# Attention steps taken as output, values, scores instead of scores, values, output

## The chip, the cores and the metric

The kernel runs on one core of a Trainium2 chip. The metric is device time in microseconds of one execution. Before the change it is 1657.19 us, the median of 10 runs from 1653.45 to 1661.23.

## The reference

A batch of 16 sequences, each of 128 tokens of width 256, goes through four layers. Each layer adds a gated cross attention over a context of the same shape and then a gated feed-forward part, all in float32:

```python
x = x + tanh(g_xattn[0]) * L0_xattn(ctx, layernorm(x), ctx)      # 16 heads of 16
x = x + tanh(g_ffn[0])   * L0_ffn(layernorm(x))                  # 8 experts, top 2, gelu
x = x + tanh(g_xattn[1]) * L1_xattn(layernorm(x), ctx, ctx)      # 16 heads of 16, biases
x = x + tanh(g_ffn[1])   * L1_ffn(layernorm(x))                  # dense plus 8 LoRA experts
x = x + tanh(g_xattn[2]) * L2_xattn(ctx, ctx, layernorm(x), mask)  # 16 heads of 16, key mask
x = x + tanh(g_ffn[2])   * L2_ffn(layernorm(x))                  # 8 experts, top 2, swiglu, and a shared one
x = x + tanh(g_xattn[3]) * L3_xattn(ctx, layernorm(x))           # 8 heads of 64, keys of both
x = x + tanh(g_ffn[3])   * L3_ffn(layernorm(x))                  # 8 experts, top 2, silu
```

An attention is the projection of queries, keys and values, scores, a softmax over the keys (in layer 1 over the other axis of the scores), the product with the values, and an output projection. Only the order in which the sequences of an attention pass through these parts is changed.

## The kernel before

**Stages.** The residual x lies in the core's memory as 16 tiles of 128 x 256, one per sequence (b). Four sequences make a block (blk), and layer norm, the query and key projections and the routers work on blocks, with 512 tokens at once. The program runs: attention of layer 0 with part of its experts' slots, the rest of these slots, attention of layers 1 and 2 in one loop (the feed-forward part of layer 1 goes along with it), the shared expert and the slots of layer 2, attention of layer 3, and its slots. A slot is 128 tokens that go to one expert.

**The attention loop.** `attend` (from L1303) walks over steps, one per sequence, in three parts. `scores` (L1184 for layers 0 to 2, L1970 for layer 3) projects the values of sequence b (`ps_v`, L942 or L948), copies them out on VectorE, multiplies keys and queries on TensorE into four PSUM banks (`ps_s`, L1212), and takes exp of the four banks on ScalarE into four tiles `e` (L1222, L1227); in layer 1 VectorE also sums e (L1236), inverts the sums and scales the values. `values` (L1255, L1995) multiplies e with the values and, in layers 0, 2 and 3, with ones for the sums (`ps_o`, L1267, in layer 3 `ps_sum` too, L2002); then VectorE takes a reciprocal (L1278, L2011) and a product (L1280, L2021) into `oT`. In layer 1 ScalarE only copies (L1275). GpSimd adds the reciprocals to a running sum (L1081), with which the program later checks that none was out of range. `output` (L1284, L2027) projects oT (`ps_y`, L1288, L2031), adds it to x on VectorE (L366) and starts the statistics of x there (L245, L246).

At iteration n the loop calls scores of step n, values of step n-1, and output of step n-2, in this order. On TensorE, ScalarE and VectorE the program's order is the order of execution (`IN_ORDER`, L1299): an instruction that waits holds up all behind it on its engine.

**Jobs between the parts.** Each part calls `tick` at certain points: scores three times (after the values' copy, halfway through the scores' matmuls, after exp), values twice (before and after the end of its vector work), output once at its end. A tick lets every running job (a Python generator) go on to its next yield, after as many ticks as it asked for. Jobs are the preparation of the next block (`ahead`, at every fourth n: layer norm, transposes, queries, keys), and what follows a finished block (`behind`, after the output of its fourth sequence: the router of a mixture layer, or layer 1's whole feed-forward part). With n equal to the number of steps, `late` is set and a filler starts, a longer job of expert matmuls (slots of layer 0, the shared expert of layer 2, slots of layer 3), which runs on behind the attention. At a block's begin, the loop runs ticks until the block's preparation is done.

**Buffers.** Four PSUM banks (pool `ps_mm`, L100) hold the scores; four more (pool `ps_x`, L101) go in turn to everything else: values projection, values, output, transposes, query and key projections. A new user waits until the user four allocations before is done with its bank. There are nine tiles `e`, three tiles for the values of a sequence, and two of `oT`.

## Time and profile before

| what | us |
|---|---|
| median of 10 runs | 1657.19 |
| the profiled execution | 1657.35 |
| its span, first to last instruction | 1655.5 |
| TensorE busy | 1538.0 (93%) |
| VectorE busy | 876.2 (53%) |
| ScalarE busy | 636.9 (38%) |
| GpSimd busy | 327.1 (20%) |

In this profile PE is TensorE, PEld its loading of weights, DVE VectorE, ACT ScalarE, POOL GpSimd and SP the queue that issues most DMAs. L with a number is a line of the kernel. "ps_y L1288 <- DVE oT" says that the instruction of line 1288 that writes ps_y waited for VectorE's writing of oT. The attention steps of layer 0 lie between 21 and 161 us of the span, those of layers 1 and 2 between 447 and 730, and those of layer 3 between 1248 and 1495. [...]

### The profile page before, as it was taken

How to read it: one execution, taken by the hardware profiler on the slowest of the kernel's cores; microseconds unless marked ns; L12 is line 12 of the kernel's file. 1: busy time of each engine (PE TensorE's matmuls, PEld its weight loads, DVE VectorE, ACT ScalarE, POOL GpSimd, SP SyncE). 2: the span in 40 equal slices, each digit the busy share in tenths (PEclk: the TensorE clock that was granted, in tenths of full speed). 3: DMA queues.
4: the chain of work that ended last, by engine and by line, in shares of the span. 5: the costliest groups of instructions: out<-in, count | busy, mean ns of one | idle time of the engine just before them, and what ended most of it. 6: DMA issues, size and time to landing. Idle time of an engine off the chain costs nothing.

```text
span 1655.5 us, 34913 instructions
## 1 busy us (share of the span) xinstructions
PE 1538.0 (93%) x12803; PEld 1195.9 (72%) x12803; DVE 876.2 (53%) x2850; ACT 636.9 (38%) x1517; POOL 327.1 (20%) x412
## 2 busy tenths in 40 slices
PE   6998999999988999999999999999989999998891
PEld 4677889999455666655559999999846665677791
DVE  3676322422367756764445555556724535557664
ACT  4455423345355555553225333334543323222110
POOL 4123411111600000221100111011150002023433
PEclk8998999999999999999999999999989999999996
DMA  9606575342600000110064414310360000034855
GB/s 337 232 28 217 187 255 171 127 145 89 118 2 1 1 15 14 40 40 26 26 219 151 152 42 139 118 33 28 100 118 1 14 1 27 1 115 133 279 171 185
DMA packets 111273, 169.68 MB, mean 102 GB/s; under 512 B 17130, under 2 KB 84527, under 8 KB 111089
## 3 DMA queue, kind: packets, MB, share of 16 engines
q1 hardware_dynamic: 86224, 112.38, 21.6%
q0 software_dynamic: 20304, 49.66, 9.5%
q10 hardware_dynamic: 4560, 5.25, 1.0%
q8 instruction: 108, 1.77, 0.5%
q14 instruction: 77, 0.62, 0.1%
HBM read 268.81 MB, written 48.18 MB: 191 GB/s over the span
## 4 chain that ended last, share of the span: by engine, by line
PE 58%; DVE 8%; ACT 4%; DMA 3%; issue 1%; POOL 0%; SPq 0%; DVEq 0%; POOLq 0%; ACTq 0%
PE ps_w L1598 16%; PE ps_w L1533 6%; PE ps_qk L1855 5%; PE ps_e L823 5%; PE ps_v L1964 3%; PE ps_g L1646 2%; PE ps_u L1646 2%; PE ps_s L1985 2%; PE ps_o L1267 2%; PE ps_y L2031 2%; PE ps_s L1555 2%; PE ps_o L2002 1%; DVE sums L1236 1%; PE ps_router L413 1%; PE ps_q L933 1%
## 5 line engine op out<-in xcount | busy, mean ns | idle before, releaser
L1598 PEld LDWEIGHTS ps_w<-xT,w 128*128 128x128 f32 x2304 | 264.0, 192 | 2.5
L1598 PE MATMUL ps_w<-xT,w 128*128 128x128 f32 x2304 | 264.9, 275 | 0.0
L835 POOL DMA_INDIRECT yd<-y,to x117 | 119.2, 1019 | 560.0 <-DVE c L798 306.9
L823 PE MATMUL ps_e<-w,hT 128*128 128x256 f32 x848 | 197.6, 380 | 2.2 <-DVE hT L1503 1.3
L823 PEld LDWEIGHTS ps_e<-w,hT 128*128 128x128 f32 x848 | 154.5, 190 | 21.4 <-DVE hT L1503 2.3
L1606 ACT ACTIVATE u<-ps_w,b 128x128 f32<-128x128 f32 x312 | 89.5, 368 | 172.5 <-PE ps_w L1598 165.3
L1609 DVE SCALAR_TENSOR_TENSOR m<-ps_w,b,u 128x128 f32<-128x128 f32 x312 | 87.8, 345 | 110.9 <-PE ps_w L1598 93.9
L1421 PE MATMUL ps_h<-xT,w 128*128 128x128 f32 x1120 | 134.9, 280 | 6.3 <-DMA w<-in_l_w_dram 4.1
L1421 PEld LDWEIGHTS ps_h<-xT,w 128*128 128x128 f32 x1120 | 132.9, 196 | 9.4 <-issue 3.8
L1426 ACT ACTIVATE hT<-ps_h,b 128x128 f32<-128x128 f32 x312 | 89.3, 373 | 117.1 <-issue 83.4
L524 POOL DMA_INDIRECT xg<-xn,xi x96 | 94.1, 980 | 153.6 <-ACT u L1539 55.0
L1533 PE MATMUL ps_w<-xnT,sw 128*128 128x512 f32 x256 | 111.8, 593 | 0.0
L831 DVE SCALAR_TENSOR_TENSOR y<-ps_e,c,bias 128x256 f32<-128x256 f32 x78 | 37.7, 483 | 125.5 <-PE ps_e L823 124.3
L1081 POOL TENSOR_TENSOR sum_range<-sum_range,rs 128x256 f32<-128x256 f32 x48 | 35.2, 733 | 343.9 <-DVE rs L1278 157.5
L1533 PEld LDWEIGHTS ps_w<-xnT,sw 128*128 128x128 f32 x256 | 47.9, 190 | 57.3 <-issue 50.9
L1278 DVE RECIPROCAL rs<-ps_o 128x256 f32<-128x256 f32 x32 | 56.2, 1756 | 45.5 <-PE ps_o L1267 43.6
L306 ACT ACTIVATE xn<-x,nmr,rstd 128x256 f32<-128x256 f32 x128 | 67.8, 598 | 31.1 <-DVE nmr L302 30.3
L788 DVE COPY xT<-ps_xr 128x256 f32<-128x256 f32 x117 | 48.6, 418 | 57.4 <-PE ps_xr L786 57.3
L1212 PE MATMUL ps_s<-qM,kT 32*128 32x256 f32 x768 | 68.9, 421 | 5.6 <-ACT e L1227 5.6
L1227 ACT ACTIVATE e<-ps_s 128x512 f32<-128x512 f32 x128 | 65.8, 602 | 11.4 <-PE ps_s L1212 11.4
L815 ACT ACTIVATE bias<-b,c 128x256 f32<-128x256 f32 x78 | 40.4, 518 | 67.0 <-DVE c L801 26.6
L1855 PE MATMUL ps_qk<-kvx,w_att 128*128 128x512 f32 x128 | 62.9, 625 | 0.6 <-DVE kvx L1842 0.6
(276 smaller groups left out, 2559.5 us busy)
## 6 DMA issues: line engine op xcount, KB each, us to landing
w<-in_l_w_dram SPq DMA_DIRECT2D x156, 1024.0 KB
w<-in_l_w_dram SPq DMA_DIRECT2D x39, 512.0 KB
kT<-in_l_wgu_dram SPq DMA_DIRECT2D x39, 512.0 KB
xg<-zeros POOLq DMA_DIRECT2D x15, 1170.0 KB, 25.6
xr<-xg SPq DMA_DIRECT2D x78, 130.0 KB
b<-in_l_b_dram SPq DMA_DIRECT2D x78, 128.0 KB
kT<-in_l_w_dram SPq DMA_DIRECT2D x39, 256.0 KB
x<-yd POOLq DMA_DIRECT2D x48, 128.0 KB, 4.8
```

The lines of the kernel that those rows point to most:

```text
L306: nc.scalar.activation(xns[:, i, 0:D], src, AF.Identity, bias=nmr[:, i:i + 1], scale=rstd[:, i:i + 1])
L524: self.unordered(nc.gpsimd.indirect_dma_start(out=xg[:, :], in_=xns[:, i, :], in_offset=None, out_offset=bass.IndirectOffsetOnAxis(ap=xi[: ...
L823: nc.tensor.matmul(po, lhsT=hT[:, f, :], rhs=lane(s)["w2"][:, f, :], start=(f == 0), stop=(f == nf - 1),)
L835: self.unordered(nc.gpsimd.indirect_dma_start(out=yd[:, :], in_=y, in_offset=None, out_offset=bass.IndirectOffsetOnAxis(ap=to[:, 0:1], axi ...
L1212: nc.tensor.matmul(pss[j][:, 2 * c:2 * c + 2, :], lhsT=self.kT[blk][part, c, tok], rhs=self.qM[blk][part, c, :, tok], start=True, stop=True,)
L1421: nc.tensor.matmul(ps[:, i, :], lhsT=w["w1"][:, k, f * P:(f + 1) * P], rhs=xT[:, k, :], start=(k == 0), stop=(k == KC - 1),)
L1426: nc.scalar.activation(hT[:, f, :], ps[:, i, :], AF.Gelu, bias=w["b1"][:, f:f + 1])
L1533: nc.tensor.matmul(ps, lhsT=wt[:, k, f * P:(f + 1) * P], rhs=xnT[:, k, :], start=(k == 0), stop=(k == KC - 1),)
L1598: nc.tensor.matmul(ps[:, f, :], lhsT=wt[:, k, s, f * P:(f + 1) * P], rhs=xT[:, k, :], start=(k == 0), stop=(k == KC - 1),)
L1606: nc.scalar.activation(u[:, f, :], pair[0][:, f, :], AF.Identity, bias=w["b1"][:, i:i + 1])
L1609: nc.vector.scalar_tensor_tensor(m1[:, f, :], pair[1][:, f, :], w["b3"][:, i:i + 1], u[:, f, :], ALU.add, ALU.mult,)
L1855: nc.tensor.matmul(ps, lhsT=w[:, k, c * P:(c + 1) * P], rhs=src[:, k, :], start=(k == 0), stop=(k == KC - 1),)
```

## The change

The three parts of an iteration come in the opposite order, and with one more step between them: output of step n-3, values of step n-2, scores of step n. The loop runs one iteration longer, and the point from which the filler runs moves by one iteration. A block's preparation still starts, and is still waited for, at the head of the iteration, which is now ahead of output and values instead of directly ahead of scores; what follows a finished block now starts between output and values.

```diff
-            for n in range(len(steps) + 2):
+            for n in range(len(steps) + 3):
                 if n == len(steps) - 1 and open_end:
                     next(filler)
-                if n == len(steps):
+                if n == len(steps) + 1:
                     late = True
...
+                if n >= 3:
+                    att, b = steps[n - 3]
+                    att.output(b, tick)
+                    if b % BPB == BPB - 1:
+                        _, _, behind, blk = blocks[(n - 3) // BPB]
+                        jobs.append([behind(blk), 0])
+                if 2 <= n < len(steps) + 2:
+                    att, b = steps[n - 2]
+                    att.values(b, tick)
+                if n < len(steps):
                     att, b = steps[n]
                     att.scores(b, tick)
-                if 1 <= n <= len(steps):
-                    att, b = steps[n - 1]
-                    att.values(b, tick)
-                if n >= 2:
-                    att, b = steps[n - 2]
-                    att.output(b, tick)
-                    if b % BPB == BPB - 1:
-                        _, _, behind, blk = blocks[(n - 2) // BPB]
-                        jobs.append([behind(blk), 0])
```

## The prediction

> **What bounds the kernel now.** I read the busy time by stretch first, for the four attention stages, since the change touches nothing else. The columns are the stretch, its length, and busy microseconds with instruction counts for TensorE, its weight load, VectorE, ScalarE and GpSimd; then granted clock, DMA share and GB/s.

> ```profile
> 21.00:161.00 140.00, 126.44 (x1634) 95.56 (x1634) 94.18 (x296) 72.55 (x152) 32.42 (x39) 0.91 0.52 192
> 434.00:584.00 150.00, 133.44 (x1118) 83.40 (x1122) 101.40 (x274) 77.11 (x164) 18.29 (x30) 0.95 0.10 15
> 584.00:730.00 146.00, 140.77 (x1707) 96.65 (x1704) 94.06 (x265) 79.37 (x140) 27.34 (x32) 1.00 0.10 31
> 1248.00:1498.00 250.00, 242.31 (x2603) 161.21 (x2602) 130.15 (x363) 75.19 (x153) 27.79 (x35) 0.99 0.10 30
> ```

> These are layers 0, 1, 2 and 3. TensorE is idle for 13.6, 16.6, 5.2 and 7.7 us of them: 43 us is all that a reordering could win, and layers 2 and 3 have almost nothing to give. So I next read what ends TensorE's waits (total, times, longest).

> ```profile
> PE ps_ln L329 <- ACT xn L306: 13.9, 8, 4.3
> ...
> PE ps_s L1212 <- ACT e L1227: 5.6, 4, 2.6
> ...
> PE ps_o L1267 <- DVE oT L1280: 3.3, 4, 1.8
> ...
> PE ps_y L1288 <- ACT oT L1275: 1.7, 2, 0.9
> ```

> The first is layer norm of the next block (part of it at 434, before the attention steps); the second, scores waiting for banks that exp still reads. The last two are not data waits: values and output wait for one of the four general PSUM banks, which an earlier values result occupies until oT is written. Adding the smaller rows of that kind (ps_l 1.4, ps_q 1.0 and 0.6 behind VectorE's oT; ps_ln 1.9, ps_zT 0.8 behind ScalarE's) gives 10.7 us. No row has output waiting for its own oT. The timeline of one step of layer 2 tells why (start, length, engine, line, operation):

> ```profile
> 619.65 1.15 PE L1212 MATMUL ps_s<-qM,kT 32*128 32x256 f32 x16
> ...
> 620.73 1.08 PE L1267 MATMUL ps_o<-e,v 128*32 128x128 f32 x32
> ...
> 621.62 1.06 PE L1267 MATMUL ps_o<-e,ones 128*32 128x128 f32 x32
> 622.61 1.13 PE L1288 MATMUL ps_y<-w_att,oT 128*128 128x256 f32 x4
> 622.82 1.76 DVE L1278 RECIPROCAL rs<-ps_o 128x256 f32<-128x256 f32 x1 [1.50 <-PE ps_o L1267]
> ...
> 623.69 1.03 PE L948 MATMUL ps_v<-w_att,ctxT 128*128 128x256 f32 x4
> 624.61 0.42 DVE L1280 TENSOR_TENSOR oT<-ps_o,rs 128x256 f32<-128x256 f32 x1
> 624.65 1.15 PE L1212 MATMUL ps_s<-qM,kT 32*128 32x256 f32 x16
> ```

> Scores, values, output follow each other. From the last values matmul (622.68) to oT written (625.03) is 2.35 us, and that oT is used only after another output, scores and values: at 628.92.

> **The change, part by part.** Nothing is added or removed but an iteration; the numbers of instructions stay. Written out, the old order is S(n) V(n-1) O(n-2) S(n+1) V(n) O(n-1), the new one S(n) O(n-2) V(n-1) S(n+1) O(n-1) V(n). So despite "two" and "three steps ago", what happens is that O and V change places. From exp to values the way grows by one output; from values to output it shrinks from O+S+V to S alone. The steps themselves issue no DMA. POOL's addition of the range watch (0.73 us, one a step) moves with values, and no engine waits for it. The queues of SP and POOL are touched otherwise only through jobs (loads, scatters) that start up to three ticks earlier relative to S, which I cost at nothing: the DMA share is 0.52 in layer 0 and 0.10 after it, and POOL is busy under a quarter of the time; without that cover it would be the 0.52 us that a late row cost at 142.32.

> (a) *Output waits for its own oT.* 2.35 us of VectorE against the scores step in between: in layer 2 from 623.69 to 625.80, 2.11 us, so 0.24 us of wait; in layer 0 the values projection is shorter (121.14 to 122.83, 1.69 us), so 0.66. That holds where no job's matmuls stand between V and O. In the new TensorE order that is 6 steps of layer 0 and 5 of layer 2: 6 x 0.66 + 5 x 0.24 = 5.2 us. Queued behind the waiting output is V(n-1), all of whose inputs are there. Bounds: 2.6 (half covered by other late work) to 11 (each wait 1 us, as output's VectorE tail, 0.48 + 0.43 + 0.18, now stands ahead of the reciprocal).

> (b) *Vector work of the router ahead of the reciprocal.* At 118 to 123 the ranks' nine small operations (about 0.19 each, 1.7 us) delayed it. In the new order such a group falls into the middle of values, where the second half (1.0 us) covers part: 0.8 us in two steps without matmul filler, 1.6. Bounds 0 and 5.0 (twice the 2.52 us from 120.24 to 122.76).

> (c) *The ends of layers 0, 2 and 3.* After the last scores the order is O(13) V(14) O(14) V(15) O(15): O(14) stands directly behind V(14), with no S between, and waits the whole 2.35 us in layers 0 and 2; in layer 3 it is about 0.8, since the reciprocal there runs under values (1264.81 to 1265.58 for the multiply). For layer 0 I take half: the expert work that follows waited there anyway (0.52 us at 142.32 for its rows). 1.2 + 2.35 + 0.8 = 4.3, bounds 0.8 and 5.5. O(15) is covered by a slice of filler (eight passes over the shared expert's weights took 3.54 us at 714.78).

> (d) *Layer norm against exp.* Jobs advance by ticks, so their place among the steps moves: the four normalizations (0.52 each, 2.08) now come ahead of a step's four exps, not behind, and exp frees the score banks later. Walking one block of layer 0 with these durations I get waits of 1.0 (next block's queries) and 0.9 (the job behind), for scores and transposes, and of 0.6 together in layer 2, where a step is longer; for three blocks that is 5.7 and 1.8 us. Against that, the present waits at these places go: 0.85, 0.66, 0.99, 1.73 and 0.88 in layer 0 (5.1) and 0.72 in layer 2. Net +1.7, bounds -5.8 and +8.

> (e) *Layer 1.* Its stalls come from a chain through both other engines: the sums of exp (2.46 us on VectorE), the statistics behind them, then ScalarE, whose oT copy stands in line behind the logarithm that waits for these. Per block before: 0.87 + 0.36 + 1.87 = 3.1 us (485 to 491). In the new order the same chain costs output and transposes some 0.9 + 0.8 to 2.4. For four blocks I take -3, bounds -8 and +6.

> (f) *Layer 3.* 242.31 of 250 us busy, oT 2 us ahead of the scores' end: 0, bounds -2 and +3.

> Where (a) and (d) fall into one step, exp catches up during output's wait: -2. The sum is 5.2 + 1.6 + 4.3 + 1.7 - 3 - 2 = +7.8 us. The profiled execution took 1657.35 (span 1655.5 and 1.85 around it), 0.16 from the median of 1657.19, so the sum gives 1665.

> **Clock.** The values step at 105.69 took 3.25 us to 108.94, the one at 113.23 only 1.96; before the slow one stands a wait of 1.73. A half-speed stretch thus cost 1.3 us, with waits of under 2 us around. Three such stretches more or fewer make 4 us either way: I put that into the range, not the sum. [...]

> **Rivals.** *Faster, 22%:* the change frees banks. Output's bank is emptied before the reciprocal occupies VectorE, so fewer of the four are held. If all 10.7 us of bank waits behind oT go and new waits stay at (a), 5.2, the time is 1651.9. For: these waits exist, above all in layer 1. Against: layer 2, with the same order, has under 3 us of them. It decides once new waits total under 7.4. *Nothing measurable, 15%:* one wait takes another's place, TensorE's idle time stays near 43 us: 1657. "About 0.2%, 3.3 us" is what a measurement of this kernel can tell. *VectorE becomes the bound, 12%:* where its queue is full (the reciprocal started 2.5, 3.1, 5.97 us late in steps of layer 0, and in seven steps of layers 0 to 2 oT was written 1.8 to 2.8 us after the scores behind which output now stands), output waits about 3 us each time: 7 x 3 = 21 us, 1678. Against: in such stretches the rest of TensorE's queue waited too.

> **How the numbers follow.** The forecast, slower by 3.3 to 16, has 51%. Slower is 51 + 12 = 63%, the same 15%, faster 22%. The range 1652 to 1678 leaves out about one in ten on each side: below, the faster rival with more than its price; above, the VectorE rival beyond its price. The likeliest case alone covers 1660.5 to 1674.

> **What would show it.** TensorE waits named output behind oT, VectorE's in layers 0 and 2, several of 0.2 to 0.7 and two of about 2.3 at the ends; the waits behind oT at other matmuls fewer; layer 2's idle time above 8 us; layer 3's the same. I would be wrong if jobs' matmuls fill the gap between V and O more often than I count, or if layer 1's chain shortens by more than a few microseconds.

## The result

The changed kernel takes **1671.03 us** (median of 9 runs, 1668.64 to 1674.48); the kernel before, beside it, 1656.27 (median of 31, 1652.69 to 1663.71). The ratio is **1.0093, 95% interval 1.0080 to 1.0106**: slower by 14.8 us. The forecast was 1665, with 63% on slower; time and sign held. The sum behind it did not hold in its parts, as the experiments show.

**Profile after.** The span is 1667.9 us, 12.4 longer than before. The busy time by stretch, over the same four windows and with the same columns as shown of before:

```profile
21.00:161.00 140.00, 119.70 (x1589) 87.58 (x1588) 94.19 (x285) 65.94 (x138) 32.43 (x39) 0.91 0.52 192
434.00:584.00 150.00, 130.53 (x1030) 78.82 (x1030) 93.16 (x252) 76.90 (x161) 23.27 (x35) 0.93 0.15 22
584.00:730.00 146.00, 141.14 (x1670) 97.89 (x1670) 96.09 (x274) 78.17 (x140) 23.58 (x29) 0.99 0.08 25
1248.00:1498.00 250.00, 244.63 (x2468) 154.77 (x2468) 122.82 (x325) 75.74 (x157) 29.17 (x37) 0.99 0.10 26
```

The windows stand still while the work moves later, so fewer instructions fall into them. Layer 0 shows the change without that: TensorE is busy 119.7 of 140 us, where it was 126.4, and gets 1589 matmuls done instead of 1634. The waits of TensorE say why (total, times, longest):

```profile
PE ps_y L1288 <- DVE oT L1280: 13.9, 14, 3.0
...
PE ps_ln L329 <- ACT xn L306: 8.0, 4, 2.7
PE ps_y L1288 <- DVE sm_m L380: 5.8, 3, 2.5
...
PE ps_y L1288 <- ACT oT L1275: 4.4, 3, 2.8
...
PE ps_s L1212 <- ACT e L1227: 2.4, 2, 2.0
PE ps_y L2033 <- DVE oT L2023: 2.2, 1, 2.2
...
PE ps_y L1288 <- DVE fm_m L398: 1.5, 1, 1.5
...
PE ps_ln L329 <- ACT oT L1275: 1.1, 1, 1.1
```

Five of these rows are output (`ps_y`), 27.8 us together; before, the rows of output came to 2.7 us (2.1 in layers 0 to 2, 0.6 in layer 3), and none was for its own oT. Where the row names `sm_m` or `fm_m`, a small router operation that stands just behind oT on VectorE, it is the same wait: in the timeline below, of layer 2, output starts at 734.11, 0.14 after oT ends at 733.97.

```profile
731.75 1.76 DVE L1278 RECIPROCAL rs<-ps_o 128x256 f32<-128x256 f32 x1 [0.92 <-PE ps_o L1267]
733.54 0.43 DVE L1280 TENSOR_TENSOR oT<-ps_o,rs 128x256 f32<-128x256 f32 x1
733.88 0.18 DVE L380 TENSOR_REDUCE sm_m<-logits 128x4 f32<-128x32 f32 x1
```

```profile
730.53 1.08 PE L1267 MATMUL ps_o<-e,ones 128*32 128x128 f32 x32
734.11 2.04 PE L1288 MATMUL ps_y<-w_att,oT 128*128 128x256 f32 x4 [2.50 <-DVE sm_m L380]
```

Three things went the other way. Of the 10.7 us of waits for a PSUM bank behind an older oT only the 1.1 of the last row above are left (9.6 gone; against that, other matmuls now wait 4.9 us in four rows behind output's addition to x, `DVE x L366`, before 0.4 in one); layer norm's 13.9 became 8.0, and scores behind exp 5.6 became 2.4. So in these rows 27.8 came and 18.7 went, +9.1. TensorE's idle time from the first scores of layer 0 to the last gating matmul of layer 3 says the same: 71.7 us before, 80.6 after (+8.9). The rest of the 12.4 is longer busy time. In sum the clock has no part in it: the time at half clock in that stretch is 68.3 us in both profiles.

For the experiments I use the length of stages, each taken between named instructions, so that it does not depend on where the work lies: layer 0 from its first scores matmul to its last output matmul; layers 1 and 2 with the shared expert from the first scores to the last `ps_w` of the shared expert; layer 3 from the first scores to the last `ps_g` of its slots. Where layers 1 and 2 are named apart, the cut is the end of layer 1's last output matmul. In brackets is the time in which TensorE runs nothing, where it is used. All are of one profiled execution each.

| kernel | layer 0 | layers 1 and 2, shared | layer 3 and its slots |
|---|---|---|---|
| before | 130.0 (12.6) | 411.5 (23.3) | 371.3 |
| after | 135.3 (19.6) | 426.3 (28.1) | 363.4 |

### The profile page after: what moved, and what is told of

Same layout as the page of the kernel before. It is cut to its first block, busy times and chain, and to the rows that moved or that the text cites. A ratio compares the mean times of both kernels' runs of the same rounds, so it can differ in the third digit from the quotient of the medians.

```text
span 1667.9 us, 34882 instructions
## 1 busy us (share of the span) xinstructions
PE 1542.6 (92%) x12803; PEld 1194.9 (72%) x12803; DVE 880.4 (53%) x2850; ACT 633.9 (38%) x1513; POOL 327.1 (20%) x412
## 3 DMA queue, kind: packets, MB, share of 16 engines
q1 hardware_dynamic: 86224, 112.38, 21.3%
## 4 chain that ended last, share of the span: by engine, by line
PE 80%; DVE 11%; DMA 3%; ACT 3%; issue 2%; SPq 1%; POOL 0%; DVEq 0%; ACTq 0%; POOLq 0%
PE ps_w L1600 15%; PE ps_e L823 12%; PE ps_h L1423 7%; PE ps_w L1535 6%; PE ps_qk L1857 5%; PE ps_o L1267 4%; PE ps_v L1966 3%; PE ps_y L1288 2%; PE ps_s L1212 2%; PE ps_s L1987 2%; DVE rs L1278 2%; PE ps_g L1648 2%; PE ps_k L933 2%; PE ps_y L2033 2%; PE ps_router L413 2%
## 5 line engine op out<-in xcount | busy, mean ns | idle before, releaser
L823 PEld LDWEIGHTS ps_e<-w,hT 128*128 128x128 f32 x848 | 154.5, 190 | 22.2 <-DVE hT L1505 2.3
L306 ACT ACTIVATE xn<-x,nmr,rstd 128x256 f32<-128x256 f32 x128 | 68.4, 595 | 45.0 <-DVE nmr L302 45.0
L1288 PE MATMUL ps_y<-w_att,oT 128*128 128x256 f32 x192 | 59.3, 435 | 25.6 <-DVE oT L1280 13.9
L1278 DVE RECIPROCAL rs<-ps_o 128x256 f32<-128x256 f32 x32 | 56.1, 1752 | 30.2 <-PE ps_o L1267 30.1
L1212 PE MATMUL ps_s<-qM,kT 32*128 32x256 f32 x768 | 69.5, 418 | 2.4 <-ACT e L1227 2.4
L1227 ACT ACTIVATE e<-ps_s 128x512 f32<-128x512 f32 x128 | 65.7, 599 | 10.7 <-PE ps_s L1212 10.5
L1288 PEld LDWEIGHTS ps_y<-w_att,oT 128*128 128x128 f32 x192 | 35.6, 205 | 46.5 <-issue 19.7
```

Source lines behind the costliest of these rows:

```text
L823: nc.tensor.matmul(po, lhsT=hT[:, f, :], rhs=lane(s)["w2"][:, f, :], start=(f == 0), stop=(f == nf - 1),)
L1212: nc.tensor.matmul(pss[j][:, 2 * c:2 * c + 2, :], lhsT=self.kT[blk][part, c, tok], rhs=self.qM[blk][part, c, :, tok], start=True, stop=True,)
L1278: nc.vector.reciprocal(rs, po[:, 1])
L1288: nc.tensor.matmul(py, lhsT=oT[:, k, :], rhs=self.w[3][:, k, :], start=(k == 0), stop=(k == KC - 1 and self.bias is None),)
```

## The experiments

In these texts theory A is the prediction's: output now waits for its own oT, and the places of the jobs matter little. Theory B, the rival, is that the places of the jobs, and VectorE's queue with them, make the difference, whatever output waits for.

### The two halves of the change, each alone

The change swaps values and output in the cycle, and it also starts a block's preparation three ticks earlier, ahead of two parts of the cycle that used to come before it. Each can be had alone. The swap alone keeps the preparation directly ahead of scores (in all these diffs `value_step(i)` and `out_step(i)` stand for the old lines that call values and output of step i):

```diff
                 if n < len(steps):
                     att, b = steps[n]
                     att.scores(b, tick)
-                if 1 <= n <= len(steps):
-                    value_step(n - 1)
                 if n >= 2:
                     out_step(n - 2)
+                if 1 <= n <= len(steps):
+                    value_step(n - 1)
```

> Output and values change places (scores n, output n-2, values n-1), while a block's preparation still starts directly ahead of scores, as before the change. Theory A, the output waits for its own oT because only one scores step lies between: the place of the preparation matters little, the time is that of the changed kernel within 4 us (1667 to 1675), and output's waits behind oT (L1288) total over 15 us. Theory B, the loss comes from the jobs' new place among the steps: without that move the time falls back to 1653 to 1661.

The earlier preparation alone keeps the cycle scores, values, output and only begins the iteration, at whose head the preparation starts, at values:

```diff
-            for n in range(len(steps) + 2):
+            for n in range(len(steps) + 3):
...
+                if 2 <= n < len(steps) + 2:
+                    value_step(n - 2)
+                if n >= 3:
+                    out_step(n - 3)
                 if n < len(steps):
                     att, b = steps[n]
                     att.scores(b, tick)
-                if 1 <= n <= len(steps):
-                    value_step(n - 1)
-                if n >= 2:
-                    out_step(n - 2)
```

> Scores, values, output keep their order in the cycle, but an iteration begins with values n-2, output n-3, so that a block's preparation starts and is waited for ahead of them, as in the changed kernel. Theory A: no output has to wait for its own oT, 1653 to 1661, with under 4 us of waits at L1288. Theory B: the jobs' place costs most of the 15 us, 1666 to 1675.

Measured beside the kernel before (1656.55): the swap alone **1690.29**, ratio 1.0185 (1.0140 to 1.0230); the earlier preparation alone **1636.95**, ratio 0.9870 (0.9841 to 0.9898), faster than either kernel. Both theories missed both times, though the waits came as theory A had them (over 15 us in the rows of L1288 in the first, 0.4 in the second). The swap costs some 34 us and the earlier preparation gives some 20; together +14, and the whole change measured +14.8. So the two add up, and the prediction's 7.8 was the difference of two numbers that it had both far too small.

The waits of TensorE in the swap alone:

```profile
PE ps_y L1288 <- DVE oT L1280: 13.5, 13, 3.0
PE ps_y L1288 <- ACT oT L1275: 10.6, 5, 4.0
...
PE ps_y L1288 <- DVE sm_m L380: 5.0, 2, 2.5
```

and with the earlier preparation alone:

```profile
PE ps_ln L329 <- ACT xn L306: 11.4, 5, 4.3
...
PE ps_s L1212 <- ACT e L1227: 4.9, 3, 2.6
...
PE ps_o L1267 <- DVE oT L1280: 1.6, 4, 0.5
...
PE ps_y L1288 <- DVE have L602: 0.4, 1, 0.4
```

The swap has the waits for oT; those of layer 1 are 10.6 us, against 4.4 with the whole change. The other has none for its own oT, and of the bank waits behind oT it has left 1.6 here and 1.0 and 0.6 in two smaller rows, 3.2 of 10.7.

| kernel | layer 0 | layers 1 and 2, shared | layer 3 and its slots |
|---|---|---|---|
| swap alone | 138.4 (21.3) | 435.6 (37.9) | 366.7 |
| earlier preparation alone | 122.8 (8.8) | 401.3 (15.3) | 367.8 |

The gain of the earlier preparation is in layer 0 (-7.2) and in layers 1 and 2 (-10.2). Of these 17.4 us, 11.8 are idle time, and in layer 0 TensorE also spent 17.1 us at half clock instead of 23.9, worth at most 3.4 (an estimate: half of the difference; in the trace of before the 32 matmuls of values' first half took 1.94 us at 105.69, at a granted clock of 0.50, and 1.08 at 113.23, at 1.00). Layer 3 and its slots are 3.5 shorter, and what lies between these stages came out some 4 longer; this profiled execution (1640.89) was the slowest of the four.

### The new order in some layers only

Here `attend` takes the new order in layer 3 alone (`open_end` is set there), or in layers 1 and 2 alone (`len(parts) == 2` in its place), and the old one elsewhere.

```diff
+            new = open_end
...
+                if new:
+                    if n >= 3:
+                        out_step(n - 3)
+                    if 2 <= n < len(steps) + 2:
+                        value_step(n - 2)
                 if n < len(steps):
                     att, b = steps[n]
                     att.scores(b, tick)
+                if not new:
...
```

> The new order in layer 3 alone; layers 0 to 2 as before. In the two traces the part from the last matmul of layer 2's slots to the last of layer 3's shrank by 9 us (22.2 us behind, then 13.0). Theory A1, this gain belongs to the order of layer 3: 1645 to 1650. Theory B1, it comes from the later start of layer 3 (what the DMA queues and the free-running clock then do), or from layers 0 to 2: 1655 to 1660, the same as before.

> The new order in the loop of layers 1 and 2 alone. Theory A: these layers carry the 14.6 us that the two traces show between the last matmul of layer 0's slots (7.6 behind) and that of layer 2's shared expert (22.2 behind), and nothing is given back later: 1668 to 1674. Theory B1, that the gain in layer 3 follows from a later start: 1659 to 1664.

### Does the wait make the cost? A shorter reciprocal

The two cycle orders were compared with the reciprocal (1.76 us, 32 times) replaced by a multiplication, which took 0.42, so that the softmax of layers 0 and 2 is not divided by its sums:

```diff
-                nc.vector.reciprocal(rs, po[:, 1])
+                nc.vector.tensor_scalar(rs, po[:, 1], 400.0, None, ALU.mult)
```

> The rotated order (values, output, scores) with the reciprocal at L1278 (1.76 us, 32 of them in layers 0 and 2) replaced by a multiplication by a constant, so the softmax of these layers is not divided by its sums; the rest of the work is as it was. The price of the nearest row, the multiplication at L1280 of the same shape, is 0.43 us. It is the reference for the next run. Theory A (the swap costs because outputs wait for their own oT, behind the reciprocal): in this order nothing waits for oT by more than 1.6 us in all, so the shorter reciprocal brings little through that wait, 1625 to 1637. Theory B (the swap costs through VectorE's queue and the places of the jobs, whatever the output waits for): 42 us less of VectorE's work brings more, 1610 to 1630.

> The new order (output, values, scores) with the same multiplication in place of the reciprocal at L1278. With the reciprocal the two orders stand 34 us apart (1671.0 against 1637.0: layer 0 12.5, layer 1 8.2, layer 2 16.8, the slots of layer 3 4.6 back). Theory A: without it the waits of layers 0 and 2 go, layer 1 (which has no such reciprocal) keeps its 8 and layer 3 its 4.6 back: 4 to 14 us above the rotated order with the short reciprocal. Theory B: the difference stays, 25 to 36 us.

These and the next two ran on a chip where the kernel before takes 1701.52, so only the ratios and the differences among them count. Short reciprocal in the rotated order: 1690.30, ratio 0.9926 (0.9902 to 0.9950), which is 1644 on the chip of 1656 and above what either theory expected. In the new order: 1701.29, ratio 1.0006 (0.9982 to 1.0030). The difference of the medians is 11.0 us, inside A's 4 to 14 and far from B's 25 to 36; the two profiled executions lie 16.8 apart, just outside. Waits for nothing that the profile shows, of which that chip has many (see the end), come to 26.0 and 35.7 us in the two, so some of the difference may be theirs. By stage it lies where A put it: layer 1, which has no such reciprocal, keeps 8.0 (150.6 against 142.6; with the reciprocal, on the other chip, 8.2), layer 0 falls from 12.5 to 5.6, and layer 2 with the shared expert from 16.8 to 7.8. The cut between layers 1 and 2 does not fall at the same work in both orders: with the new one, one step's values (64 rows of TensorE; a float32 matmul call shows two rows, as the two calls of L1288 show x4) and four more query rows, by their lengths some 4 us, lie behind layer 1's last output. So some 4 of layer 2's 16.8, and of its 7.8, belong to layer 1; together the two layers go from 25.0 to 15.8. The waits of the new order with the short reciprocal, in the row of the output matmul (busy and mean ns of one, then idle time before it and its causes):

```profile
L1288 PE MATMUL ps_y<-w_att,oT 128*128 128x256 f32 x192 | 57.5, 425 | 9.8 <-ACT oT L1275 4.4 <-DVE oT L1280 2.8 <-DVE sm_m L380 2.3
```

The 4.4 of layer 1 is unchanged; VectorE's rows at this line go from 21.2 to 5.4 (9.8 - 4.4). One thing I can't place: 42.6 us less of VectorE's work brought the rotated order nothing in the ratio (0.9926, on the other chip 0.9870 with the long reciprocal). The two chips differ in more than the clock, so I draw nothing from that.

### The ends of the layers

The new order, but values ahead of output again once the last scores are out:

```diff
+                if n < len(steps):
                     if n >= 3:
                         out_step(n - 3)
                     if n >= 2:
                         value_step(n - 2)
+                else:
+                    if n < len(steps) + 2:
+                        value_step(n - 2)
+                    out_step(n - 3)
```

> The new order, but once the last scores of a group of layers are out (the last two steps of layers 0, 2 and 3), values come ahead of output again. Prediction's term for these ends was 4.3 us: by it 1667. Theory A with the waits of the changed kernel's trace (layer 0's last four outputs waited 1.34, 2.99, 2.50 and 1.91, layer 2's last two 2.50 and 1.55, layer 3's last 2.2): about half of those 15 us goes, 1661 to 1667. Theory B (the ends are no part of it, the place of the jobs along the whole layer is): 1669 to 1673.

1715.71, ratio 1.0076 (1.0052 to 1.0101), on the chip of 1701.52. Against 1.0093 for the whole change that is 0.17%, some 3 us, and the intervals overlap: the size of the ends is not settled by this run. It agrees with the prediction's 4.3, but with anything from a small loss to some 9 us as well; the point itself (1669) lies nearer to theory B than to A. The waits did go: in its trace the last two outputs of layers 0 and 2 and the last one of layer 3 that waited, 10.7 us together in the changed kernel, wait no more. What they cost the whole is what stays open.

### A whole cycle between values and output

The new order kept, but in layers 0, 2 and 3 with the output of four steps ago:

```diff
-                if n >= 3:
-                    out_step(n - 3)
+                for i in (n - 3, n - 4):
+                    if 0 <= i < len(steps) and n - i == (
+                        3 if len(parts) == 2 and i < B else 4
+                    ):
+                        out_step(i)
```

> The new order, but in layers 0, 2 and 3 the output is that of four steps ago: a whole cycle of output, values and scores lies between a step's values and its output, so that no output can wait for its own oT, while output still comes ahead of values in the program and the jobs start in the same place. Layer 1 as in the changed kernel. Theory A: layers 0 and 2 lose what the swap cost them (12.5 and 16.8), less a later end of each by one step's residual: 1641 to 1652. Theory B: 1667 to 1675.

> The kernel with the output of four steps ago in layers 0, 2 and 3 once more, beside the two others: in its first run layer 2 with the shared expert was 17.3 us shorter than with the new order on the same chip (267.4 against 284.7) and no output of layers 0 and 2 waited, but layer 0 came out 7.6 longer at half clock for 34 us. Theory A (the waits for oT are the swap's cost, and that layer 0 was the clock of one chip): 1641 to 1652, a ratio of 0.991 to 0.997. Theory B (a later output costs layer 0 what the waits cost, since its weights and its layer norm come later): the ratio stays at 0.998 to 1.002.

First 1700.28, ratio 0.9985 (0.9965 to 1.0005), on the chip of 1701.52; then 1652.28, ratio 0.9974 (0.9958 to 0.9990), beside a kernel before of 1656.80. No output of the three layers waits for its own oT any more, as meant (in the second run one of layer 0 waited 1.10 us and began 0.15 after a later step's oT; in the first none did), and layer 1 keeps its 4.4:

```profile
PE ps_h L1431 <- DMA w<-in_l_w_dram: 8.5, 3, 3.3
PE ps_xr L786 <- DMA xr<-xg: 5.6, 2, 5.3
PE ps_y L1288 <- ACT oT L1275: 4.4, 3, 2.8
```

Both ratios lie between their two expectations (the first is 1654 on the chip of 1656), and the stages (of the second run) tell why: each theory is right somewhere. Layer 2 with the shared expert goes from 275.5 to 260.2, so 15.3 us come back with the wait alone, the cycle, the preparation and the work between the cuts being as in the changed kernel; the swap cost 16.8 there by the cuts, some 13 by the work. Of the 15.3, 8.5 are idle time and up to 3.4 the half clock that went with it. Layer 3 goes from 244.7 to 236.2 up to its last output, with 0.5 us of idle time, but its slots take 4.4 longer (123.1 against 118.7). In layer 0 the last scores come 6.9 earlier than in the changed kernel (124.6 against 131.5), but then the first experts' rows and weights are waited for, as the two DMA rows show:

```profile
132.49 0.93 PE L329 MATMUL ps_ln<-ident,xn 128*128 128x128 f32 x4 [1.56 <-ACT xn L306]
138.69 0.66 PE L786 MATMUL ps_xr<-ident,xr 128*128 128x128 f32 x2 [5.27 <-DMA xr<-xg]
142.66 3.75 PE L1431 MATMUL ps_h<-xT,w 128*128 128x128 f32 x16 [3.31 <-DMA w<-in_l_w_dram]
```

and the layer with its slots ends only 1.2 earlier. These matmuls stand ahead of the last two outputs (154.18 and 156.94 in that trace), so the layer's end waits for them too.

### By degrees: the preparation one tick early

Against the kernel with the earlier preparation, its start moves back from before values to between values and output:

```diff
+                if 2 <= n < len(steps) + 2:
+                    value_step(n - 2)
                 if n < len(steps):
                     if n % BPB == 0:
...
                             prepared = ahead(att, before, blk)
-                if 2 <= n < len(steps) + 2:
-                    value_step(n - 2)
                 if n >= 3:
                     out_step(n - 3)
```

> The rotated order with the next block's preparation started between values and output: two ticks later than in the rotated order, one tick earlier than in the kernel before. Theory A (the rotation's 20 us are the preparation's place among the steps, by degrees): between the two, 1640 to 1652, ratio 0.990 to 0.998. Theory B (one place, that ahead of values, decides, since the vector work must be behind them): as before, 1652 to 1660, ratio above 0.998.

1651.00, ratio 0.9965 (0.9946 to 0.9984), beside 1656.80. Theory A's "by degrees" held in the medians: one tick earlier gives about 6 us, three give 20. Its layer 0 took 124.0 us, between 130.0 before and 122.8, and its layers 1 and 2 with the shared expert 403.6, between 411.5 and 401.3. So in this profiled execution, the fastest of the ten (1644.47), one tick already brought 13.9 of the 17.4 us of these stages: how the gain is spread over the three ticks is not settled.

### The parts put together

Two kernels take the earlier preparation in layers 0 to 2 and another order in layer 3: the first the new order, the second (4 in place of 3 in the two lines of layer 3, and one iteration more there) the new order with the output of four steps ago.

```diff
+                if open_end and n >= 3:
+                    out_step(n - 3)
                 if 2 <= n < len(steps) + 2:
                     value_step(n - 2)
-                if n >= 3:
+                if not open_end and n >= 3:
                     out_step(n - 3)
```

> The rotated order (values, output, scores) in layers 0, 1 and 2 and the new order (output, values, scores) in layer 3 alone. If the parts add up (rotated: 19.6 us less than before; the new order in layer 3 alone: 3.7 us less, most of it in the slots behind that layer, where the rotated order had 0.9 less): about 1634, 1629 to 1638, a ratio of 0.983 to 0.989. If the slots' gain of the new order in layer 3 hung on what the earlier layers left behind: 1637 to 1642.

> The rotated order in layers 0, 1 and 2, and in layer 3 alone output of four steps ago, then values of two steps ago, then new scores. In the last run layer 3 with this later output took 236.2 us with 0.5 of TensorE's waits (244.7 in the changed kernel, 246.9 with the new order in layer 3 alone) and its slots 123.1 (119.9). If layer 3's own waits for oT and for VectorE cost it that, and what the layers before left behind does not matter: 7 us below the last kernel (1634.3), 1624 to 1631, a ratio of 0.980 to 0.984. If those 8 us came from the state in which layers 0 to 2 left the chip: 1632 to 1638.

The first took **1634.31**, ratio 0.9869 (0.9847 to 0.9891), beside 1656.80: as expected, 22 us faster than the kernel before and 37 faster than the changed one. Against the earlier preparation alone (1636.95, ratio 0.9870) it is no measured gain; layer 3 and its slots took 366.8 instead of 367.8. The second missed both its expectations: 1694.37, ratio 0.9923 (0.9900 to 0.9946), on a chip where the kernel before takes 1709.14. Layer 1 came out as in the first kernel to a tenth (142.8), but layer 3 did not get the 236.2 us (247.3, with 10.2 at half clock), and stages whose order is the same in both took longer (layer 2 with the shared expert 281.2 against 258.7). What that chip did is told at the end; whether the later output in layer 3 is worth anything on the chip of the other runs stays open.

## Why the prediction was right, and where it was not

- **What bounds it.** Right. The kernel's time followed TensorE's waits in the attention stages, and the new waits were those named: output behind oT, because output and values change places.
- **(a) Output's own wait.** Right in size: 7.3 us where the sum had 5.2. Layer 2's plain steps waited 0.27, 0.27, 0.27 and 0.28 where the working said 0.24, and layer 0's 0.24 to 1.34 where it said 0.66. The row of one of them, with scores in front as counted:

```profile
718.23 1.15 PE L1212 MATMUL ps_s<-qM,kT 32*128 32x256 f32 x16
719.18 0.42 DVE L1280 TENSOR_TENSOR oT<-ps_o,rs 128x256 f32<-128x256 f32 x1
...
719.66 1.13 PE L1288 MATMUL ps_y<-w_att,oT 128*128 128x256 f32 x4 [0.28 <-DVE oT L1280]
```

- **(b) Router work ahead of the reciprocal.** The mechanism was right, the size wrong: 5.4 us in two steps (2.99 in layer 0, 2.44 in layer 2) where the sum had 1.6, just beyond its upper bound of 5.0. The sum counted nine small operations and let values' second half cover part of the group. In layer 2 it covered nothing: that half ended at 707.29, the thirteen small operations of the expert choice stood between 707.05 and 709.67 on VectorE, and the reciprocal behind them began at 709.59.

```profile
709.26 0.19 DVE L405 TENSOR_TENSOR hot<-fm_rk,fm_rm 128x32 f32<-128x32 f32 x1
709.48 0.19 DVE L464 TENSOR_TENSOR both<-hot 128x32 f32<-128x32 f32 x1
...
709.59 1.75 DVE L1278 RECIPROCAL rs<-ps_o 128x256 f32<-128x256 f32 x1
...
711.86 1.13 PE L1288 MATMUL ps_y<-w_att,oT 128*128 128x256 f32 x4 [2.44 <-DVE oT L1280]
```

- **(c) The ends.** Named rightly, sized at less than half. The last two outputs of layer 0 waited 2.50 and 1.91, those of layer 2 2.50 and 1.55, and O(14) of layer 3 2.24: 10.7 us where the sum had 4.3 and an upper bound of 5.5. Halving layer 0's share was wrong, and so was the belief that a filler slice covers O(15). In layer 3 the sum had 0.8 for the multiplication alone, but six small operations of the expert choice (1497.21 to 1498.75) stood between the reciprocal and it on VectorE. What these waits cost the end of the program is less sure, since the run with the old order at the ends won only about 3.
- **(d) and (e) The places of the jobs, and layer 1.** This is the step that failed. (d) walked one block and came to +1.7, (e) took -3 for layer 1: together -1.3. The earlier preparation alone is worth -20, -7.2 of it in layer 0 and -10.2 in layers 1 and 2. The faster rival had the largest piece of the idle time in it, the 10.7 us of bank waits (7.5 went with the earlier preparation alone, which has 13.0 less idle time), and its point of decision was right too: with the whole change 9.6 went, and the change lost because the new waits were 27.8, not under 7.4. In layer 1 output waited 4.4 us, and the chain was nearly as (e) described it: the sums of exp on VectorE, then layer norm's statistics, then ScalarE, whose copy of oT stands behind the normalization that waits for them (the prediction had the logarithm there). The longest of the three waits:

```profile
464.55 2.47 DVE L1236 TENSOR_REDUCE sums<-e 128x4 f32<-128x512 f32 x4 [0.99 <-ACT e L1227]
...
468.59 1.09 ACT L306 ACTIVATE xn<-x,nmr,rstd 128x256 f32<-128x256 f32 x2 [2.61 <-DVE nmr L302]
469.58 0.35 ACT L1275 COPY oT<-ps_o 128x256 f32<-128x256 f32 x1
...
469.98 2.07 PE L1288 MATMUL ps_y<-w_att,oT 128*128 128x256 f32 x4 [2.83 <-ACT oT L1275]
```

- **(f) Layer 3.** The layer itself came out 2.4 us shorter, a little beyond the lower bound of -2, but the sum looked only at the attention: the slots behind it became 5.5 us shorter.
- **The swap's cost.** The prediction's (a), (b) and (c) made 11.1 us of new waits; they were 27.8 in the whole change, and the swap alone cost 34. Eight waits of 1.5 to 3.0 us make 19.0 of the 27.8. That is near the VectorE rival's seven waits of 3 us, but five of the eight stand at the ends, which (c) had named. Against the earlier preparation alone the changed kernel's profile is longer by 28.9: idle time is +10.8 in layer 0 and +12.8 in layers 1 and 2, and half-clock time +3.4 and +13.7, worth at most half of that, 8.6 us. Against the kernel before, to which the range's 4 us for the clock belong, the half-clock time did not change in sum: -3.4 in layer 0, +13.7 in layers 1 and 2, -10.3 in layer 3 and its slots.
- **Why it came out right.** The cost was underrated by some 23 us and the gain by some 18. The time lay in the range because these errors met, not because the terms were good.

That the waits for oT make the swap's cost is shown in layer 2 (15.3 us came back with the later output, 9.0 with the shorter reciprocal) and, up to the last scores, in layer 0. In layer 1 it is only argued from the chain above. Why the earlier preparation helps is shown as far as its place goes, by degrees, and by the bank waits that go; which of its vector operations matter was not tried.

## What to carry to other kernels

In a software pipeline on engines that run in program order (in the changed kernel the values matmuls at 713.03, whose exp had ended at 707.85, stood behind the output that waited until 711.86), write the cycle out and measure, for each product, the time from its last input to its use: the kernel before had a whole output, scores and values between oT and its use, and the change left scores alone against 2.35 us of VectorE. A loop's head is part of the order: moving what starts there by three ticks was worth more than any one row of waits in view, so do such a shift alone before judging a reordering that includes it. When a sum of small terms of both signs agrees with the measured time, run the halves apart before believing the terms.

## What the runs showed of the hardware

**The clock fell after some waits of about 2.5 us.** No wait of layer 2 in the changed kernel is longer than 2.50. The busy time by windows of about 3.5 us around two of them (the granted clock is the third number from the end):

```profile
704.70:708.10 3.40, 3.40 (x72) 2.65 (x70) 3.09 (x15) 2.91 (x5) 0.16 (x1) 1.00 0.02 5
708.10:711.50 3.40, 1.32 (x18) 0.72 (x16) 3.16 (x11) 2.00 (x3) 0.01 (x1) 1.00 0.00 0
711.50:715.00 3.50, 3.14 (x38) 2.36 (x38) 2.36 (x10) 0.79 (x2) 0.72 (x1) 0.73 0.00 0
...
730.00:733.50 3.50, 1.61 (x38) 1.32 (x37) 1.94 (x2) 0.00 (x0) 2.87 (x4) 1.00 0.58 211
733.50:737.00 3.50, 2.89 (x6) 1.87 (x7) 1.60 (x6) 0.23 (x1) 0.99 (x2) 0.51 0.11 38
737.00:741.00 4.00, 4.00 (x40) 1.95 (x38) 1.25 (x4) 0.69 (x1) 0.00 (x0) 1.00 0.00 0
```

A stretch in which TensorE was busy for 1.32 of 3.40 or 1.61 of 3.50 us is followed by one at 0.73 or 0.51. The two half-clock records there are 3.41 us long each; in the first, the 32 matmuls of values' first half took 1.91 us (713.03), behind it 1.08 (720.83). So by the estimate above up to 1.7 us more are lost behind such a wait. In the second run of the kernel with the later output, layer 2's steps have no wait above 0.7 and no half clock at all. A wait alone does not decide it: in the changed kernel's trace one of 3.03 us, up to 1523.14 in layer 3's slots, was followed by full clock:

```profile
1519.40:1522.80 3.40, 0.71 (x4) 0.28 (x2) 1.66 (x9) 1.59 (x3) 2.49 (x4) 1.00 0.74 182
1522.80:1526.20 3.40, 3.06 (x24) 2.87 (x25) 3.21 (x16) 3.11 (x7) 2.52 (x3) 1.00 0.38 140
```

What tells the two cases apart was not tried.

**Some chips were slower in a way of their own.** Where the kernel before took 1701 and 1709 us, TensorE shows waits of up to about 1 us between matmuls, for instance in the middle of values (the last kernel, in layer 2):

```profile
682.93 0.44 PE L1267 MATMUL ps_o<-e,ones 128*32 128x128 f32 x5 [0.31 <-issue]
684.40 0.42 PE L1267 MATMUL ps_o<-e,ones 128*32 128x128 f32 x3 [1.03 <-issue]
685.84 0.43 PE L1267 MATMUL ps_o<-e,ones 128*32 128x128 f32 x4 [1.02 <-issue]
```

"issue" is a wait for nothing that the profile shows. These waits came to 8.3 us in that layer; in the run of 1634.31 such halves of values ran through in 1.06 to 1.08 us. Values (L1267) has 7.5 to 15.1 us of them in each of the five traces from these chips and none in the others. The granted clock of the profiled executions was lower there too, 0.955 to 0.958 against 0.967 to 0.975. In that stretch, 681 to 688.4, the DMA engines were 0.53 busy, but the cause was not tried. A ratio to a kernel run beside it does not take this out, since it strikes some orders more than others (between layer 0's first scores and layer 3's last gating matmul 24.1 us of such waits with the later output, 35.7 with the new order and the short reciprocal).
